# A graph-attention layer with residual and layer norm: adjacency loads by whole blocks, x loads one step later and singly near the end, statistics ahead of normalisation

## The chip, the core and the metric

The kernel runs on one core of a Trainium2 chip. A core has five engines that run their own instruction streams and meet through semaphores: TensorE (PE in the profile; its weight loads are PEld), VectorE (DVE), ScalarE (ACT), GpSimd (POOL) and SyncE (SP, which here only issues DMAs). Data comes from HBM into SBUF, an on-chip memory of 128 partitions; TensorE writes its results to PSUM. The metric is the device time of one execution in microseconds; the number compared is the median over runs.

## The reference

The inputs are x (4096 x 512), adj (4096 x 4096), W (512 x 2048: four heads of 512) and a (the heads' attention vectors), all float32.

```
ht  = (x @ W) by heads
e   = leaky_relu(src_i + dst_j, 0.01) + adj        # src = ht . a_src, dst = ht . a_dst
att = softmax(e over j)
y   = mean over heads of att @ ht
out = layernorm(x + y)        # mean and variance over 512, eps 1e-5, no scale, no shift
```

The entries of adj that aren't zero lie between 0.05 and 1e9. In nearly every row the largest entry of adj exceeds the second by so much more than the attention scores can differ that the softmax is exactly one at that entry and zero elsewhere. Then `att @ ht` for row i is `x[col_i] @ W_h`, where `col_i` is the place of the largest entry of the row, and the mean over heads is `x[col_i] @ mean(W_h)`. The kernel computes this, and a bound which proves it for these inputs.

## The kernel before

Rows are handled in 32 blocks of 128: partition p holds the rows 32p to 32p+31, and block `ib` is row 32p+ib of every partition. One block of adj is 128 x 4096 float32, 2 MB, 16 KB in each partition.

**Buffers.** `adj_pool` has six buffers of one block each. `hold` (128 x 32 x 512, L95) keeps all of x, and later the output in its place; while W is needed, the second half of `hold` holds W (L96, `load_w`). Four PSUM banks are for `o`, the sum of a block's residual and product, and two for transposes.

**Loads.** All of them are issued by SyncE in order. `load_adj` (L105) loads a block in pieces: `pieces` (L102) gives four for block 0 and for blocks 28 to 31, and two for the others. `load_x` (L112) loads four blocks of x at a time. Step t of the main loop (from L352) issues x if it is due, then block t+5 of adj; `x_at` (L347) puts group g, blocks 4g to 4g+3, at step 4g-2, ahead of block 4g+3 of adj. After the loop comes the last group of x (blocks 28 to 31), then the stores of blocks 0 to 25, still from SyncE. A load into an adj buffer waits until VectorE has read the block that was in it, and every DMA of SyncE waits until the one eight issues before it has landed.

**The work on one block, spread over seven steps.** At step t:
- VectorE finds the largest entry of each of 64 segments of 64 columns of block t (`segment_maxima`, L155, one reduction for each piece), and then the best segment (`find_segment`, L162 and L164). Between the two halves of the block it does `find_column` (L184, L189) for block t-2: the place inside the segment.
- GpSimd computes the row index (L166), gathers the best segment of each row from HBM (`lead`, L168), and for block t-2 the column (L191) and with it the 128 rows of x (`y`, L178).
- TensorE transposes the gathered rows of block t-3 (`turn`, L204), which ScalarE copies to SBUF (`yt`, L206), starts the sum with the residual (identity times x, `residual`, L210), and multiplies by the mean of W (`products`, L217; `w_sum` is made in the first three steps).
- ScalarE takes the mean and the variance of block t-4 (`stats`, L229 and L231), and the squared length of its x rows (`row_norm`, L224), for the bound.
- Every second step GpSimd turns the sums of two blocks, t-6 and t-5, into a factor and a shift (`rstd`, L234 to L236, which writes `sd` and `nm`), and ScalarE normalises the two into `hold` (`finish`, L240). In before, ScalarE has the order: copy of `yt`, `finish` of the pair, `stats`, `row_norm`.
- In steps 1 to 14 TensorE and ScalarE also make the attention vectors (L279 to L287), which step 16 turns into norms (`head_norms`).

**The end.** Blocks 28 to 31 are normalised by VectorE (`finish_last`, L246 to L255: add, bn_stats, bn_aggr, a square root on ScalarE, reciprocal, scaling). `bound` needs the squared lengths of all rows: part 0 takes the maximum over blocks (`xm`, L312) and transposes it on TensorE (L314), part 1 reduces it, takes the root and spreads it (L316 to L319), part 2 forms the limit; `test`, `count` and `report` compare all rows with it. Each engine works through its instructions in the order of the program text, which is written out by hand:

```
    row_norm(28 .. 31)                           # ScalarE
    turn(NB - 2)
    products(NB - 3, KB - 1, KB)
    bound(0)
    products(NB - 2)
    finish_last(NB - 4, True)
    find_inner(NB - 1)
    bound(1)
    finish_last(NB - 3, True)
```

The program text by line numbers:

Of the kernel before, what the change touches and what calls it, by code (L numbers as in the profile page):

```python
# [65 lines left out]
def leading_rows(ctx, tc, x, adj, W, a, out, ident, v, n_bad, any_bad):  # L66
# [7 lines left out]
    nc = tc.nc  # L74
    N, D = x.shape
    H = a.shape[0]
    KB, NB, S = D // P, N // P, N // E
    AHEAD = 5
    Q = 4
    PIECES = 4  # L80
    LATE = NB - Q
# [9 lines left out]
    x_rows = x.rearrange("(p nb) d -> p nb d", nb=NB)  # L91
# [3 lines left out]
    hold = once.tile([P, NB, D], F32, name="hold")  # L95
# [4 lines left out]
    adj_t = {}  # L100

    def pieces(ib):  # L102
        return PIECES if ib == 0 or ib >= LATE else PIECES // 2

    def load_adj(ib):  # L105
        if 0 <= ib < NB:
            t = adj_t[ib] = adj_pool.tile([P, N], F32, name="adj_t")
            n = pieces(ib)
            for k in range(n):
                nc.sync.dma_start(t[:, ts(k, N // n)], adj_rows[ib][:, ts(k, N // n)])  # L110

    def load_x(g):  # L112
        nc.sync.dma_start(hold[:, ts(g, Q), :], x_rows[:, ts(g, Q), :])

    def load_w(kb):
        nc.sync.dma_start(hold[:, ds(w_at + kb * H, H), :], w_blocks[:, kb])
# [4 lines left out]
    for kb in range(KB):  # L121
        load_w(kb)
        load_adj(kb + 1)
    load_x(0)
    for ib in range(KB + 1, AHEAD):
        load_adj(ib)

# [21 lines left out]
    def segment_maxima(ib, lo, hi):  # L149

        if lo == 0:
            seg_of[ib] = small.tile([P, S], F32, name="seg")
        n = pieces(ib)
        for k in range(lo * n // PIECES, hi * n // PIECES):
            nc.vector.tensor_reduce(  # L155
                seg_of[ib][:, ts(k, S // n)],
                adj_t[ib][:, ts(k, N // n)].rearrange("p (s e) -> p s e", e=E), axis=AX.X, op=OP.max,
            )

    def find_segment(ib):  # L160
        seg = seg_of.pop(ib)
        nc.vector.max(out=top[:, ib, :], in_=seg)  # L162
        at = small.tile([P, 8], U32, name="at")
        nc.vector.max_index(at, top[:, ib, :], seg)  # L164
        row = small.tile([P, 1], U32, name="row")
        nc.gpsimd.tensor_tensor(row, at[:, 0:1], first[:, ib : ib + 1], op=OP.add)  # L166
        lead = small.tile([P, E], F32, name="lead")
        nc.gpsimd.indirect_dma_start(  # L168
            out=lead, out_offset=None, in_=adj_segs,
            in_offset=bass.IndirectOffsetOnAxis(ap=row[:, :1], axis=0),  # L170
        )
        start = at_of[ib] = small.tile([P, 1], U32, name="start")
        nc.gpsimd.tensor_tensor(start, at[:, 0:1], width, op=OP.mult)  # L173
        lead_of[ib] = lead
# [8 lines left out]
    def find_inner(ib):  # L183
        nc.vector.max(out=inner[:, ib, :], in_=lead_of[ib])  # L184

    def find_column(ib):
        find_inner(ib)
        within = small.tile([P, 8], U32, name="within")
        nc.vector.max_index(within, inner[:, ib, :], lead_of.pop(ib))  # L189
        col = small.tile([P, 1], U32, name="col")  # L190
        nc.gpsimd.tensor_tensor(col, at_of.pop(ib), within[:, 0:1], op=OP.add)  # L191
        gather_rows(ib, col)
# [15 lines left out]
    def residual(ib):  # L208
        o_ps[ib] = psum.tile([P, D], F32, name="o")
        nc.tensor.matmul(o_ps[ib], ident, hold[:, ib, :], start=True, stop=False)  # L210

    def products(ib, lo=0, hi=KB):
        start = ib not in o_ps
        if start:
            o_ps[ib] = psum.tile([P, D], F32, name="o")
        for kb in range(lo, hi):
            nc.tensor.matmul(  # L217
                o_ps[ib], yt_of[ib][:, kb, :], w_sum[:, kb, :],
                start=(start and kb == 0), stop=(kb == KB - 1),
            )  # L220

    def row_norm(ib):
        sq = rows.tile([P, D], F32, name="sq")
        nc.scalar.activation(sq, hold[:, ib, :], AF.Square, accum_out=xx[:, ib : ib + 1])  # L224

    def stats(ib):
        o, i = o_ps[ib], slice(ib, ib + 1)
        sq = rows.tile([P, D], F32, name="sq")
        nc.scalar.activation(sq, o, AF.Identity, scale=-1.0 / D, accum_out=nm[:, i])  # L229
        sq = rows.tile([P, D], F32, name="sq")  # L230
        nc.scalar.activation(sq, o, AF.Square, bias=nm[:, i], accum_out=sd[:, i])  # L231

    def rstd(i):
        nc.gpsimd.tensor_scalar(sd[:, i], sd[:, i], 1.0 / D, EPS, op0=OP.mult, op1=OP.add)  # L234
        nc.gpsimd.tensor_tensor(sd[:, i], sd[:, i], power[:, : i.stop - i.start], op=OP.pow)  # L235
        nc.gpsimd.tensor_mul(nm[:, i], nm[:, i], sd[:, i])  # L236
# [5 lines left out]
    def finish_last(ib, residual):  # L242

        o = o_ps.pop(ib)
        if residual:
            nc.vector.tensor_add(hold[:, ib, :], o, hold[:, ib, :])  # L246
            o = hold[:, ib, :]
        st = small.tile([P, nc.vector.BN_STATS_DIM], F32, name="st", bufs=2)
        nc.vector.bn_stats(st, o)  # L249
        mv = small.tile([P, nc.vector.BN_AGGR_DIM], F32, name="mv", bufs=2)  # L250
        nc.vector.bn_aggr(mv, st)
        r = small.tile([P, 1], F32, name="r", bufs=2)
        nc.scalar.activation(r, mv[:, 1:2], AF.Sqrt, bias=eps)
        nc.vector.reciprocal(r, r)
        nc.vector.tensor_scalar(hold[:, ib, :], o, mv[:, 0:1], r, op0=OP.subtract, op1=OP.mult)  # L255
# [4 lines left out]
    def mean_of_heads(kb):  # L260
        o = psum.tile([P, D], F32, name="o")
        for h in range(H):
            nc.tensor.matmul(o, ident, hold[:, w_at + kb * H + h, :], start=(h == 0), stop=(h == H - 1))  # L263
        nc.scalar.activation(w_sum[:, kb, :], o, AF.Copy, scale=1.0 / H)  # L264
# [5 lines left out]
    def turn_a():  # L270
        tp = psum.tile([P, KB, P], F32, name="tp", bufs=2)
        for k in range(KB):
            nc.tensor.transpose(tp[:, k, : 2 * H], a_rows[:, ts(k, P)], ident[: 2 * H, : 2 * H])
        nc.scalar.copy(at_d, tp[:, :, : 2 * H])
# [33 lines left out]
    def bound(part):  # L308

        if part == 0:  # L310
            xm = once.tile([P, 1], F32, name="xm")
            nc.vector.tensor_reduce(xm, xx, axis=AX.X, op=OP.max)  # L312
            px = of_bound[0] = psum.tile([1, P], F32, name="px", bufs=1)
            nc.tensor.transpose(px, xm, ident)  # L314
        elif part == 1:
            nc.vector.tensor_reduce(xg, of_bound[0], axis=AX.X, op=OP.max)  # L316
            nc.scalar.activation(xg, xg, AF.Sqrt)
            pb = of_bound[1] = psum.tile([P, 1], F32, name="px", bufs=1)
            nc.tensor.matmul(pb, ones[0:1, :], xg, start=True, stop=True)  # L319
        else:  # L320
            nc.vector.tensor_mul(lead_by, of_bound[1], vn)
            nc.vector.tensor_scalar(lead_by, lead_by, 1.05, 110.0, op0=OP.mult, op1=OP.add)
# [21 lines left out]
        nc.vector.tensor_reduce(total, pg, axis=AX.X, op=OP.add)  # L344
        nc.vector.tensor_scalar(any_bad, total, -1.0, float(N), op0=OP.mult, op1=OP.add)

    x_at = {4 * g - 2: g for g in range(1, NB // Q - 1)}  # L347
    vectors = [(kb, h) for kb in range(KB) for h in range(H)]
    vectors_at = {t: 2 if t < 3 else 1 for t in range(1, 15)}
    COLUMN, PROJECT, STATS, FINISH = 2, 3, 4, 6  # L350

    for t in range(NB):  # L352
        if t in x_at:
            load_x(x_at[t])
        load_adj(t + AHEAD)
        middle = 1 if t == NB - 1 else 2
        segment_maxima(t, 0, middle)
        if t >= COLUMN:
            find_column(t - COLUMN)
        segment_maxima(t, middle, PIECES)  # L360
        find_segment(t)
        pair = t >= FINISH and t % 2 == 0
        if pair:
            rstd(slice(t - FINISH, t - FINISH + 2))
        if t < 2:
            mean_of_heads(t)
        elif t == 2:
            mean_of_heads(2)
            mean_of_heads(3)
        if t == 0:  # L370
            turn_a()
        turned = [(*vectors[0], turn_w(*vectors.pop(0))) for _ in range(vectors_at.get(t, 0))]
        if t == 16:
            head_norms()
        ib = t - PROJECT
        if ib >= 0:
            turn(ib)
            if ib < LATE:
                residual(ib)
        for some in turned:  # L380
            head_vector(*some)
        if ib >= 0:
            products(ib)
        if pair:
            finish(t - FINISH)
            finish(t - FINISH + 1)
        if t >= STATS:
            stats(t - STATS)
            row_norm(t - STATS)

    load_x(NB // Q - 1)
    for ib in range(NB - FINISH):
        store(nc.sync, ib, 1)
    find_column(NB - 2)
# [7 lines left out]
        row_norm(ib)  # L402
    turn(NB - 2)
    products(NB - 3, KB - 1, KB)
    bound(0)
    products(NB - 2)
    finish_last(NB - 4, True)
    find_inner(NB - 1)
    bound(1)
    finish_last(NB - 3, True)  # L410
    bound(2)
# [249 lines left out]
```

## Time and profile before

| what | value |
|---|---|
| median of 7 runs | 250.38 us (248.48 to 250.75) |
| the profiled execution | 249.54 us |
| its span (first to last instruction of the trace) | 247.6 us |
| PE, DVE, ACT, POOL busy | 80%, 76%, 44%, 39% of the span |
| bytes moved by DMA | 97.77 MB, 395 GB/s over the span |
| loads of adj by SyncE | 54 of 1 MB, 20 of 512 KB |
| loads of x by SyncE | 8 of 1 MB |
| stores | 31 by SyncE, 1 by ScalarE, 256 KB each |

The profile is of one execution, so sums of its durations are set against 249.54 us and its span, not against the median. In its lists a row is: start and length in us (or length in ns), engine, line of the program, operation, output <- inputs with their shapes, how many, and in square brackets the idle time of the engine before it and what ended it. A DMA counts from its issue to its landing. The "DMA share" is the busy share of the 16 DMA engines and can come out a little over one. TensorE's matmul ends are modelled, so its busy share says little about how near it is to its peak.

### The profile page before, as it was taken

How to read it: one execution, taken by the hardware profiler on the slowest of the kernel's cores; microseconds unless marked ns; L12 is line 12 of the kernel's file. 1: busy time of each engine (PE TensorE's matmuls, PEld its weight loads, DVE VectorE, ACT ScalarE, POOL GpSimd, SP SyncE). 2: the span in 40 equal slices, each digit the busy share in tenths (PEclk: the TensorE clock that was granted, in tenths of full speed). 3: DMA queues.
4: the chain of work that ended last, by engine and by line, in shares of the span. 5: the costliest groups of instructions: out<-in, count | busy, mean ns of one | idle time of the engine just before them, and what ended most of it. 6: DMA issues, size and time to landing. Idle time of an engine off the chain costs nothing.

```text
span 247.6 us, 2569 instructions
## 1 busy us (share of the span) xinstructions
PE 199.1 (80%) x677; PEld 99.9 (40%) x678; DVE 188.9 (76%) x304; ACT 110.0 (44%) x266; POOL 97.5 (39%) x213
## 2 busy tenths in 40 slices
PE   0098859999999999999687878887799875957970
PEld 0034526466666666555242423332343332423420
DVE  2656677696899489967989799949995899973681
ACT  2002002144747575657555453645193708294310
POOL 1022423245256524654454546344554445563000
PEclk9999799999999999999999999999799999999996
DMA  6999999999999999999999999999999999999991
GB/s 242 418 417 420 418 414 412 417 413 410 417 408 408 408 418 413 412 413 410 416 409 417 406 417 408 408 411 410 417 412 408 403 404 401 405 398 356 398 342 65
DMA packets 20612, 97.77 MB, mean 395 GB/s; under 512 B 2920, under 2 KB 2920, under 8 KB 12144
## 3 DMA queue, kind: packets, MB, share of 16 engines
q1 hardware_dynamic: 16848, 87.83, 88.0%
q0 software_dynamic: 3584, 9.44, 10.0%
q10 hardware_dynamic: 160, 0.28, 0.3%
q8 instruction: 7, 0.11, 0.2%
q14 instruction: 13, 0.11, 0.1%
HBM read 89.15 MB, written 8.39 MB: 394 GB/s over the span
## 4 chain that ended last, share of the span: by engine, by line
DMA 48%; issue 19%; POOL 19%; DVE 10%; ACT 2%; POOLq 0%; PE 0%; DVEq 0%
DMA adj_t<-in_adj_dram 38%; DMA hold<-in_L_gnn_W_dram 6%; POOL lead L168 6%; POOL y L178 6%; DVE seg L155 4%; DMA y<-in_x_dram,col 3%; POOL sd L235 2%; POOL start L173 1%; POOL row L166 1%; POOL col L191 1%; DVE st L249 1%; ACT sq L224 1%; DVE hold L255 1%; DVE hold L246 1%; POOL sd L234 1%
## 5 line engine op out<-in xcount | busy, mean ns | idle before, releaser
L155 DVE TENSOR_REDUCE seg<-adj_t 128x32 f32<-128x2048 f32 (+1 forms) x74 | 146.3, 1987 | 36.8 <-DMA adj_t<-in_adj_dram 36.8
L217 PE MATMUL o<-w_sum,yt 128*128 128x512 f32 x256 | 118.6, 605 | 5.8 <-ACT yt L206 5.8
L217 PEld LDWEIGHTS o<-w_sum,yt 128*128 128x128 f32 x256 | 46.3, 191 | 64.1 <-issue 45.6
L178 POOL DMA_INDIRECT y<-in_x_dram,col x32 | 32.2, 1007 | 17.4 <-POOL col L191 15.2
L168 POOL DMA_INDIRECT lead<-in_adj_dram,row x32 | 30.8, 963 | 15.5 <-POOL row L166 15.5
L263 PE MATMUL o<-hold,ident 128*128 128x512 f32 x32 | 19.1, 751 | 17.1 <-DMA hold<-in_L_gnn_W_dram 17.1
L206 ACT COPY yt<-tp 128x512 f32<-128x512 f32 x32 | 18.7, 585 | 29.8 <-PE tp L204 29.6
L204 PE MATMUL tp<-ident,y 128*128 128x128 f32 x128 | 20.1, 281 | 14.3 <-DMA y<-in_x_dram,col 14.2
L210 PE MATMUL o<-hold,ident 128*128 128x512 f32 x58 | 30.7, 611 | 0.5 <-DMA hold<-in_x_dram 0.5
L240 ACT ACTIVATE hold<-o,nm,sd 128x512 f32<-128x512 f32 x28 | 20.3, 777 | 23.2 <-POOL nm L236 23.2
L166 POOL TENSOR_TENSOR row<-at,first 128x1 uint32<-128x1 uint32 x32 | 5.9, 184 | 54.3 <-DVE at L164 53.2
L204 PEld LDWEIGHTS tp<-ident,y 128*128 128x128 f32 x128 | 14.7, 144 | 27.5 <-issue 27.1
L281 ACT COPY wt<-tp 128x512 f32<-128x512 f32 x16 | 9.2, 586 | 29.7 <-PE tp L279 29.7
L191 POOL TENSOR_TENSOR col<-start,within 128x1 uint32<-128x1 uint32 x31 | 5.8, 188 | 37.4 <-DVE within L189 36.6
L224 ACT ACTIVATE sq<-hold 128x512 f32<-128x512 f32 x32 | 19.8, 620 | 0.0
L231 ACT ACTIVATE sq<-o,nm 128x512 f32<-128x512 f32 x28 | 19.3, 688 | 0.9
L287 PEld LDWEIGHTS pv<-at_d,wt 128*128 128x128 f32 x128 | 16.2, 191 | 7.0 <-ACT wt L281 4.0
L263 PEld LDWEIGHTS o<-hold,ident 128*128 128x128 f32 x32 | 7.3, 238 | 26.3 <-POOL row L166 12.1
L264 ACT ACTIVATE w_sum<-o 128x512 f32<-128x512 f32 x4 | 2.4, 598 | 33.9 <-PE o L263 33.9
L229 ACT ACTIVATE sq<-o 128x512 f32<-128x512 f32 x28 | 16.9, 604 | 0.0
L287 PE MATMUL pv<-at_d,wt 128*128 128x2 f32 x128 | 15.4, 244 | 0.6 <-ACT wt L281 0.6
L279 PEld LDWEIGHTS tp<-ident,hold 128*128 128x128 f32 x64 | 7.9, 142 | 6.9 <-issue 6.9
(73 smaller groups left out, 116.7 us busy)
## 6 DMA issues: line engine op xcount, KB each, us to landing
adj_t<-in_adj_dram SPq DMA_DIRECT2D x54, 1024.0 KB, 22.5
adj_t<-in_adj_dram SPq DMA_DIRECT2D x20, 512.0 KB, 11.9
hold<-in_x_dram SPq DMA_DIRECT2D x8, 1024.0 KB, 23.0
out_dram<-hold SPq DMA_DIRECT2D x31, 256.0 KB, 4.7
hold<-in_L_gnn_W_dram SPq DMA_DIRECT2D x4, 1024.0 KB, 17.3
lead<-in_adj_dram,row POOLq DMA_INDIRECT x32, 5.6
y<-in_x_dram,col POOLq DMA_INDIRECT x32, 7.0
out_dram<-hold ACTq DMA_DIRECT2D x1, 256.0 KB, 2.5
```

Of the source, the lines that this page charges most:

```text
L155: nc.vector.tensor_reduce(seg_of[ib][:, ts(k, S // n)], adj_t[ib][:, ts(k, N // n)].rearrange("p (s e) -> p s e", e=E), axis=AX.X, op=OP.max,)
L168: nc.gpsimd.indirect_dma_start(out=lead, out_offset=None, in_=adj_segs, in_offset=bass.IndirectOffsetOnAxis(ap=row[:, :1], axis=0),)
L178: nc.gpsimd.indirect_dma_start(out=y, out_offset=None, in_=x, in_offset=bass.IndirectOffsetOnAxis(ap=col[:, :1], axis=0),)
L204: nc.tensor.transpose(tp[:, kb, :], y[:, ts(kb, P)], ident)
L206: nc.scalar.copy(yt, tp)
L210: nc.tensor.matmul(o_ps[ib], ident, hold[:, ib, :], start=True, stop=False)
L217: nc.tensor.matmul(o_ps[ib], yt_of[ib][:, kb, :], w_sum[:, kb, :], start=(start and kb == 0), stop=(kb == KB - 1),)
L224: nc.scalar.activation(sq, hold[:, ib, :], AF.Square, accum_out=xx[:, ib : ib + 1])
L231: nc.scalar.activation(sq, o, AF.Square, bias=nm[:, i], accum_out=sd[:, i])
L240: nc.scalar.activation(hold[:, ib, :], o_ps.pop(ib), AF.Identity, bias=nm[:, i], scale=sd[:, i])
L263: nc.tensor.matmul(o, ident, hold[:, w_at + kb * H + h, :], start=(h == 0), stop=(h == H - 1))
L287: nc.tensor.matmul(pv[:, kb, h : 2 * H : H], wt[:, k, :], at_d[:, k, h : 2 * H : H], start=(k == 0), stop=(k == KB - 1),)
```

## The change

Five things change.

1. Blocks 1 to 27 of adj are loaded by one DMA of 2 MB each, 29 and 30 by two; 0, 28 and 31 stay at four. VectorE still reduces each block in at least two halves (`n = max(pieces(ib), 2)`).
2. The groups of x for blocks 4 to 23 are asked for one step later (step 4g-1), and so stand behind block 4g+3 of adj in the queue instead of ahead of it.
3. x for blocks 24 to 27 comes by four loads of one block (256 KB), at steps 22 to 25, each ahead of one of the blocks 27 to 30 of adj.
4. In a step of the main loop ScalarE does `stats` and `row_norm` ahead of the pair's `finish`.
5. At the end, `finish_last` of block 28 and `find_inner` of block 31 move ahead of `bound(0)` and of the products of block 30.

```diff
     def pieces(ib):
-        return PIECES if ib == 0 or ib >= LATE else PIECES // 2
+        return PIECES if ib in (0, LATE, NB - 1) else 2 if ib > LATE else 1
...
-    def load_x(g):
-        nc.sync.dma_start(hold[:, ts(g, Q), :], x_rows[:, ts(g, Q), :])
+    def load_x(lo, n):
+        nc.sync.dma_start(hold[:, ds(lo, n), :], x_rows[:, ds(lo, n), :])
...
-        n = pieces(ib)
+        n = max(pieces(ib), 2)
         for k in range(lo * n // PIECES, hi * n // PIECES):
...
-    x_at = {4 * g - 2: g for g in range(1, NB // Q - 1)}
+    x_at = {lo - 1: (lo, Q) for lo in range(Q, LATE - Q, Q)}
+    x_at.update({ib - 2: (ib, 1) for ib in range(LATE - Q, LATE)})
...
         if t in x_at:
-            load_x(x_at[t])
+            load_x(*x_at[t])
...
+        if t >= STATS:
+            stats(t - STATS)
+            row_norm(t - STATS)
         if pair:
             finish(t - FINISH)
             finish(t - FINISH + 1)
-        if t >= STATS:
-            stats(t - STATS)
-            row_norm(t - STATS)
-
-    load_x(NB // Q - 1)
+
+    load_x(LATE, NB - LATE)
...
     products(NB - 3, KB - 1, KB)
+    finish_last(NB - 4, True)
+    find_inner(NB - 1)
     bound(0)
     products(NB - 2)
-    finish_last(NB - 4, True)
-    find_inner(NB - 1)
     bound(1)
     finish_last(NB - 3, True)
```

More of the change, by code (lines that the diff above doesn't have):

```diff
@@ L123, in leading_rows @@
         load_adj(kb + 1)
-    load_x(0)
+    load_x(0, Q)
     for ib in range(KB + 1, AHEAD):
```

## The prediction, made before the changed kernel was run

> **What bounds the kernel now.** I read the slices and DMA rows of the page first, then the busy time by stage, and then VectorE, GpSimd, ScalarE and TensorE in order of time from 190 us on. The slices:
>
> ```profile
> DMA  6999999999999999999999999999999999999991
> ...
> DMA packets 20612, 97.77 MB, mean 395 GB/s; under 512 B 2920, under 2 KB 2920, under 8 KB 12144
> ```
>
> The DMA engines never rest, so until the last block of adj has landed time is bytes. By stage (columns: window, length, busy of PE, PEld, DVE, ACT, POOL, TensorE clock, DMA share, GB/s):
>
> ```profile
> 164.00:189.70 25.70, 21.00 (x55) 9.14 (x55) 21.48 (x32) 12.91 (x32) 12.24 (x27) 0.93 1.02 413
> 189.70:216.50 26.80, 21.68 (x61) 9.28 (x60) 25.32 (x44) 13.13 (x33) 13.15 (x29) 1.00 1.03 404
> ```
>
> The first window is four blocks in 8 KB rows, with one 1 MB load of x; VectorE has 4.2 us to spare. The second holds the four last blocks in 4 KB rows without x: VectorE is nearly full and the rate falls to 404. VectorE in order of time:
>
> ```profile
> 192.93 2.29 DVE L155 TENSOR_REDUCE seg<-adj_t 128x32 f32<-128x2048 f32 x1 [0.41 <-DMA adj_t<-in_adj_dram]
> ...
> 212.85 1.20 DVE L155 TENSOR_REDUCE seg<-adj_t 128x16 f32<-128x1024 f32 x1
> ...
> 220.68 4.42 DVE L197 FIND_INDEX8 col<-top,adj_t 128x8 uint32<-128x4096 f32 x1
> 230.36 0.19 DVE L312 TENSOR_REDUCE xm<-xx 128x1 f32<-128x32 f32 x1 [5.27 <-ACT sq L224]
> ```
>
> After the second half of block 27 (192.93) it waits for no adj any more, and starts block 31 at 212.85. Then comes a 5.27 us wait for row squares. Why they are late is seen in GpSimd, then ScalarE:
>
> ```profile
> 216.78 1.06 POOL L178 DMA_INDIRECT y<-in_x_dram,col  x1 [0.39 <-POOL col L191]
> ```
> ```profile
> 225.96 0.59 ACT L206 COPY yt<-tp 128x512 f32<-128x512 f32 x1 [3.48 <-PE tp L204]
> 226.44 1.45 ACT L240 ACTIVATE hold<-o,nm,sd 128x512 f32<-128x512 f32 x2
> ...
> 230.23 0.58 ACT L206 COPY yt<-tp 128x512 f32<-128x512 f32 x1
> 232.13 0.29 ACT L253 ACTIVATE r<-mv,eps 128x1 f32<-128x1 f32 x1 [1.32 <-DVE mv L251]
> ```
>
> Block 29's rows are asked for at 216.78, 3.85 us after VectorE is done with block 30, and land at 225.16 (8.37 us, stores are under way). ScalarE copies them, normalises 26 and 27, squares four rows, and copies block 30's rows. TensorE:
>
> ```profile
> 230.60 0.27 PE L314 MATMUL px<-ident,xm 128*1 128x128 f32 x1
> 230.86 3.70 PE L217 MATMUL o<-w_sum,yt 128*128 128x512 f32 x8
> 234.49 0.38 PE L319 MATMUL px<-xg,ones 1*128 1x1 f32 x2
> 234.80 0.66 PE L204 MATMUL tp<-ident,y 128*128 128x128 f32 x4
> ```
>
> From here TensorE (block 30's products, block 31's transposes and products, done at 240.17) and VectorE (28, 29, test, 30, report, at 240.39) run without a pause and meet at block 31's bn_stats, 240.32. The last store goes out at 242.62. The stores before it drain until 242.24, so the store queue stands just behind.
>
> **What the Trainium skill says.** "DMA: Bandwidth & Descriptors", "Why small descriptors are slow (HBM only)": every packet carries a fixed cost. The trace agrees: packets of q1 take 84, 162 and 314 ns (medians) for 2, 4 and 8 KB, so 8 to 10 ns fixed. Same page, "Queues, rings and completion order": a DMA engine alternates between queues packet by packet, so a gather waits for other queues' packets. The trace agrees: y gathers take 7.0 to 7.1 us among 8 KB packets and 6.3 to 6.4 among 4 KB ones; four packets each, 4 x 0.15 = 0.6. "PSUM — Partial Sum Buffer", "Engine vs sequencer instructions": ScalarE, VectorE and GpSimd are strict FIFOs, and TensorE's matmuls keep program order; the timelines above show the same.
>
> **The change, part by part.** The bare numbers are block numbers.
>
> *Whole blocks 1 to 27.* A 16 KB row replaces two of 8 KB; no 16 KB load of adj is in the trace. If it is one packet it costs 8 + 2 x 306 = 620 ns against 628. Each engine carries 8 rows of a block: 8 x 8 ns, and one completion packet of 9 ns less, is 73 ns a block, 1.97 us by block 27. Bounds: nothing, if rows are cut to 8 KB; 3.9 us with the fixed cost from mean durations (168.1 and 319.5 give 16.7 ns: 27 x (8 x 16.7 + 9)). I take 1.97. VectorE now starts a block when all of it is there, so block results come up to 2.8 us later; mid-kernel nobody misses them. Prices: without x a block period is 5.735 us ((25.7 - 4 x 0.07 - 2.56)/4, with 8 x 0.3195 for x), VectorE needs 5.56 (66.89 to 72.45). A buffer is freed about 1.4 us before the next block has landed, with four blocks behind it in the queue: no gap. Had it only one block, each late release would cost.
>
> *x one step later, and 24 to 27 singly.* Group loads land right behind block 4g+3 instead of before it: 2.6 us after it, while block 4g's gathered rows, which TensorE transposes ahead of the residual, come some 5.5 us after it. Cost nothing, with 3 us cover. Three of the four last single loads move behind block 27: 0.75 x 2.56 = 1.92 us earlier; 2 KB rows cost 8 x (4 x 84 - 314) = 0.18 us more in all, 0.05 of it before block 27. SyncE's queue issues 43 loads of adj instead of 74 and 11 of x instead of 8, at 0.33 us each (SP rows of 0.33); it runs some 22 us ahead of the data, so that is covered. So block 27 lands at 192.91 - 1.97 - 1.87 = 189.07.
>
> *VectorE from block 27 to 31.* Before: 212.85 - 192.93 = 19.92 us from its second half. After: the whole of 27 (5.56), 28 in quarters (5.68, 195.80 to 201.48), 29 and 30 in halves (5.56 each): 22.36, which is 2.44 more. Block 30's second half lands near 208.6, when VectorE gets to it, so this is a near tie. Block 31 starts 1.97 + 1.87 - 2.44 = 1.40 earlier; I take 1.3 for the tie. Everything that follows from block 30 (lead, y of 29 and 30, ScalarE's squares) moves with it. The gather's 8.37 us I leave; it could be 7.
>
> *Statistics before the pair's normalisation.* ScalarE waits 23.2 us in all for nm; 2.3 us of statistics (L229, L231, L224) now fill that. It isn't the bound (44%). The normalisation frees the PSUM bank that the next step's residual needs; its nm is ready no earlier, and the statistics are done by then. Nothing either way; if they were late, the residual has 2.9 us in hand.
>
> *finish_last(28) before bound(0).* Add, bn_stats and bn_aggr of block 28 (1.6 us) go into VectorE's 5.27 us wait. But the square root r stands on ScalarE behind block 30's copy: r 230.75 instead of 232.13. Reciprocal, scaling and inner follow (r to inner took 0.99 before), so xm starts at 231.87 instead of 230.36. On TensorE xm's transpose stands ahead of block 30's products, which were ready at 230.81. Behind them queue the broadcast, block 31's transposes, its products: all 1.5 us later. VectorE's 0.7 us gain before block 30 is lost to waiting. End of the tail: +1.5.
>
> Sum: -1.3 + 1.5 = +0.2 us on the profiled execution (249.54, span 247.6). It lies 0.84 below the median of the runs, 250.38; I add the difference to the median: 250.6.
>
> **Rivals.** *A row of 16 KB brings nothing* (cut in two, or HBM is slower at it). Place: landing of block 27; price 1.97, so +2.2: 252.6, slower. It decides once less than about 1 us is saved. For: no such packet of adj in the trace. Against: 2, 4 and 8 KB rows are one packet each. *The front gains more*: 3.9 us saved, or block 29's gather back at 7 us because it meets the stores later: -1.3 to -1.9, less the tie: 249.1, faster. For: the mean durations, and gathers of 6.3 at 221.45. Against: the 413 and 404 GB/s fit the smaller cost. *Gathers become the wait*: behind 16 KB packets y takes 7 + 4 x 0.31 = 8.2, lead 5.5 + 0.6 = 6.1. VectorE wants lead 7.4 us after its issue (2 x 5.735 + 2.3 - 5.56 - 0.8). At 8.2 the waits use up VectorE's 3.3 us of spare per four blocks; beyond, it is late at 27, around +2: 252.4. Against: three times my estimate would be needed.
>
> **How the numbers follow.** Forecast 0.45, no gain of rows 0.20, more gain 0.25, gathers 0.10. About 0.5% (1.25 us) is what a measurement can tell from no change. Faster: 0.22 of the third and 0.03 of the first; slower: 0.18, 0.07 and 0.06; same: the rest, 0.44. Range 248.7 to 252.8; the forecast's own is 249.4 to 251.8.
>
> **What would show it.** Packets of 16 KB near 620 ns. Block 27's first reduction near 189.1, block 31's near 211.5, y of 29 asked for near 215.5. VectorE's wait for row squares split, its rest before L254 of block 28; L314 followed by products about 1.5 us after ScalarE's copy of yt. y gathers near 8.2 us in mid-kernel. Wrong if rows show as 8 KB packets, if TensorE waits for x at L210, or if block 30's rows, not r, hold L314.

## The result, and the profile after

The changed kernel takes 248.01 us in the median of 27 runs (246.84 to 250.08), against 249.53 of the kernel before (64 runs on the same chip). The ratio is 0.9939, with a 95% interval of 0.9924 to 0.9953: 1.5 us faster, where 0.2 us slower was forecast. The profiled execution took 248.13 us with a span of 246.2 (before: 249.54 and 247.6), so the two profiles show nearly the whole difference. Of the cases that the prediction named, the second rival, a front that gains more, came nearest.

The slices and the packets, on the page of the changed kernel:

```profile
DMA  6999999999999999999999999999999999999961
...
DMA packets 16580, 97.77 MB, mean 397 GB/s; under 512 B 2472, under 2 KB 2472, under 8 KB 11184
```

The same bytes go in 4,032 fewer packets. In the trace q1 has 3,456 packets of 16 KB (27 blocks of 128 rows), so a row is one packet. It takes 620 ns in the median, as forecast, and 625.5 in the mean; an 8 KB packet of the kernel before took 314 in the median and 319.5 in the mean. Before, only the very last slice was not full; now the last two are a 6 and a 1, so the stores drain well before the end.

By stage (window, length, busy of PE, PEld, DVE, ACT, POOL, TensorE clock, DMA share, GB/s), up to block 27 and from there to block 31:

```profile
162.80:188.00 25.20, 19.53 (x54) 8.01 (x52) 20.94 (x32) 13.14 (x32) 12.31 (x27) 1.00 1.01 413
188.00:214.00 26.00, 24.11 (x69) 10.74 (x70) 24.91 (x40) 15.73 (x40) 14.74 (x32) 1.00 1.02 407
```

The windows are alike in kind, and VectorE is still nearly full in the second; both just come earlier. Over the long middle the rate rises from 412 (35 to 189.7 us, before) to 417 GB/s (35 to 188 us). What had been moved when block 27 landed (packets and MB of all queues, then packets, MB and share of the time for SyncE's queue q1 and the gathers' queue q0), before, at 192.91:

```profile
DMA packets 13004, 78.52 MB, mean 407 GB/s; under 512 B 1956, under 2 KB 1956, under 8 KB 4673
...
q1 hardware_dynamic: 10113, 70.93, 90.3%
q0 software_dynamic: 2864, 7.44, 9.9%
```

and after, at 188.01:

```profile
DMA packets 9096, 77.50 MB, mean 412 GB/s; under 512 B 1503, under 2 KB 1503, under 8 KB 4349
...
q1 hardware_dynamic: 6317, 70.22, 90.0%
q0 software_dynamic: 2752, 7.15, 9.7%
```

So block 27 came sooner for two reasons: the bytes moved faster, and there were fewer of them ahead of it, of x (q1) and of the gathers (q0). VectorE in order of time:

```profile
188.03 2.29 DVE L155 TENSOR_REDUCE seg<-adj_t 128x32 f32<-128x2048 f32 x1 [0.82 <-DMA adj_t<-in_adj_dram]
...
210.44 1.20 DVE L155 TENSOR_REDUCE seg<-adj_t 128x16 f32<-128x1024 f32 x1
...
218.00 0.23 DVE L184 MAX8 inner<-lead 128x8 f32<-128x64 f32 x1 [1.80 <-DMA lead<-in_adj_dram,row]
...
224.53 0.69 DVE L246 TENSOR_TENSOR hold<-o,hold 128x512 f32<-128x512 f32 x1 [1.09 <-ACT sq L224]
...
228.11 0.16 DVE L254 RECIPROCAL r<-r 128x1 f32<-128x1 f32 x1 [1.95 <-ACT r L253]
```

Block 27 is there at 188.03, 4.9 us earlier than its last half before; block 31 is begun at 210.44, 2.41 earlier. At the end the 5.27 us wait for row squares has become 1.09, and a new wait of 1.95 stands before L254 of block 28. GpSimd, ScalarE and TensorE:

```profile
214.37 1.06 POOL L178 DMA_INDIRECT y<-in_x_dram,col  x1 [0.39 <-POOL col L191]
```
```profile
221.95 0.59 ACT L206 COPY yt<-tp 128x512 f32<-128x512 f32 x1 [2.22 <-PE tp L204]
222.43 1.45 ACT L240 ACTIVATE hold<-o,nm,sd 128x512 f32<-128x512 f32 x2
...
227.30 0.58 ACT L206 COPY yt<-tp 128x512 f32<-128x512 f32 x1 [0.97 <-PE tp L204]
227.78 0.30 ACT L253 ACTIVATE r<-mv,eps 128x1 f32<-128x1 f32 x1
```
```profile
226.63 0.63 PE L204 MATMUL tp<-ident,y 128*128 128x128 f32 x4 [1.20 <-DMA y<-in_x_dram,col]
227.09 1.02 PE L217 MATMUL o<-w_sum,yt 128*128 128x512 f32 x2
229.12 0.27 PE L314 MATMUL px<-ident,xm 128*1 128x128 f32 x1 [1.01 <-DVE xm L312]
```

Block 29's rows are asked for at 214.37 and land at 220.97: 6.60 us, where the profile before had 8.37. Its copy comes at 221.95 instead of 225.96. Block 30's rows (219.75 to 226.49) are then what TensorE and ScalarE wait for, not ScalarE's squares. From the start of block 30's copy to the start of its products it is 1.93 us (227.30 to 229.23) instead of 0.63: that is the price of the end's order.

### The profile page after: what moved, and what is told of

Read it like the earlier page. It is cut to its first block, busy times and chain, and to the rows that moved or that the text cites. A ratio compares the mean times of both kernels' runs of the same rounds, so it can differ in the third digit from the quotient of the medians.

```text
span 246.2 us, 2538 instructions
## 1 busy us (share of the span) xinstructions
PE 199.5 (81%) x677; PEld 100.4 (41%) x678; DVE 188.8 (77%) x300; ACT 110.3 (45%) x266; POOL 97.3 (40%) x213
## 4 chain that ended last, share of the span: by engine, by line
DMA 38%; issue 24%; POOL 22%; DVE 7%; PE 4%; ACT 1%; SPq 1%; POOLq 0%; DVEq 0%
DMA adj_t<-in_adj_dram 29%; POOL lead L168 7%; POOL y L178 7%; DMA y<-in_x_dram,col 6%; DVE seg L155 5%; DMA lead<-in_adj_dram,row 3%; PE o L217 3%; POOL sd L235 3%; POOL row L166 1%; POOL start L173 1%; POOL col L191 1%; PE tp L204 1%; POOL sd L234 1%; POOL nm L236 1%; DVE hold L255 1%
## 5 line engine op out<-in xcount | busy, mean ns | idle before, releaser
L217 PE MATMUL o<-w_sum,yt 128*128 128x512 f32 x256 | 119.8, 610 | 1.4 <-ACT yt L206 1.4
L263 PE MATMUL o<-hold,ident 128*128 128x512 f32 x32 | 20.6, 805 | 16.3 <-DMA hold<-in_L_gnn_W_dram 16.3
L210 PE MATMUL o<-hold,ident 128*128 128x512 f32 x58 | 29.8, 595 | 0.0
L240 ACT ACTIVATE hold<-o,nm,sd 128x512 f32<-128x512 f32 x28 | 20.2, 772 | 3.5 <-POOL nm L236 3.5
L263 PEld LDWEIGHTS o<-hold,ident 128*128 128x128 f32 x32 | 8.0, 262 | 26.3 <-POOL row L166 11.8
```

Source lines behind the costliest of these rows:

```text
L217: nc.tensor.matmul(o_ps[ib], yt_of[ib][:, kb, :], w_sum[:, kb, :], start=(start and kb == 0), stop=(kb == KB - 1),)
L240: nc.scalar.activation(hold[:, ib, :], o_ps.pop(ib), AF.Identity, bias=nm[:, i], scale=sd[:, i])
```

## The experiments

Ratios are to the kernel before, timed beside each on the same chip; medians in us. No experiment leaves out any of the computation. A second profile of the kernel before and of the changed one (the last experiment) took 249.01 and 247.96 us; where two numbers stand together below, the second is from these.

### One part of the change alone, on the kernel before

**Whole rows only**, timed twice, each time beside other kernels:

```diff
-        return PIECES if ib == 0 or ib >= LATE else PIECES // 2
+        return PIECES if ib in (0, LATE, NB - 1) else 2 if ib > LATE else 1
-        n = pieces(ib)
+        n = max(pieces(ib), 2)
```

> The kernel before with whole-block loads alone (x timing, ScalarE order and end as before). Theory: a 16 KB packet saves 13.5 ns against two of 8 KB in the mean (625.5 against 2 x 319.5), so block 27 lands 3.0 us earlier, near 189.9; from there VectorE needs 22.4 us for four blocks (19.9 before from the second half of 27), so its first reduction of block 31 starts near 212.3, only 0.5 us earlier than before, and the end moves by about -0.5 us. Rival 1, the rows are the whole gain: -1.5 us or more. Rival 2, late halves cost as much as rows save or more: 0 to +1.

> The kernel before with whole-block loads alone, once more: the first time gave a ratio of 0.9932 from 7 runs, with a profile in which TensorE's clock was halved from 220.8 to 224.2. Theory: block 27 lands near 189.9, block 31's first reduction near 212.3, and the end is 0.5 to 1.5 us earlier, the more when block 29's gather lands within 6.5 us; ratio 0.994 to 0.998. Rival, the rows give the whole of the change: ratio 0.992 to 0.994 again.

Measured: 248.41 (7 runs), ratio 0.9932 (0.9906 to 0.9958), and 248.45 (22 runs), 0.9959 (0.9940 to 0.9979). Rows alone gain 1.0 to 1.7 us. VectorE began block 27 at 190.75 and 190.12, 2.2 to 3.0 us earlier than it began the last half of it before. The edit also loads blocks 29 and 30 by halves instead of quarters, which wasn't timed apart. The expectation's 13.5 ns a row turned out too high a price (see why the prediction was wrong). The gather of block 29 took 6.24 and 5.99 us. Both profiles hold one thing more, taken up below: block 28's products, 3.70 us before, took 5.4.

**Timing of x only:**

```diff
-    x_at = {4 * g - 2: g for g in range(1, NB // Q - 1)}
+    x_at = {lo - 1: (lo, Q) for lo in range(Q, LATE - Q, Q)}
+    x_at.update({ib - 2: (ib, 1) for ib in range(LATE - Q, LATE)})
```

> The kernel before with the x timing alone (groups one step later, 24 to 27 singly). Theory: block 27 lands 1.9 us earlier, near 191.0, but the bytes up to block 31 are the same, so its pieces land where they did, and VectorE, which is done with block 30 by 211, waits for them: first reduction of block 31 near 212.3, the end -0.5 us. Each of rows and x is worth little alone, and together 2.4 (the changed kernel's first reduction of block 31 is at 210.44 against 212.85). Rival 1, x is the whole gain: -1.5. Rival 2, residuals wait for the later x: a wait at L210 of some us in all, and 0 or slower.

Measured: 249.65, ratio 1.0011 (0.9992 to 1.0031): nothing. Block 27 is there by 190.44, but with half rows the bytes of blocks 28 to 31 follow no faster, VectorE waits for pieces of them, and begins block 31 at 212.35, only 0.5 earlier.

**The end's order only:** `finish_last(NB - 4, True)` and `find_inner(NB - 1)` ahead of `bound(0)`, as in part 5 of the change.

> The kernel before with the end's order alone (finish_last of block 28 and find_inner ahead of bound(0)). Theory: the square root of 28 stands behind the copy of block 30's rows on ScalarE, xm behind it on VectorE, and block 30's products behind xm's transpose on TensorE: products start 1.9 us after that copy instead of 0.6, and the end is 1.3 to 1.5 us later. Rival, the new order fills the 5.3 us wait: 1.0 to 1.6 us earlier.

Measured: 250.58, ratio 1.0029 (1.0012 to 1.0046): slower by 0.7 us, half of what was forecast. The mechanism shows in its profile: the products of block 30 start 1.93 us after the copy of block 30's rows started, against 0.63 before. That execution took 252.55 us, the longest of the 22, and held a stretch at half clock (below) at 222.33, so nothing else is read from it.

### One part taken back from the changed kernel

**Rows in halves again** (`pieces` and `n` as before, the rest changed):

> The changed kernel with rows in halves as before (x timing, ScalarE order and end as changed). Theory: block 27 lands near 191.0 or a little before, VectorE is then held by block 31's pieces, whose bytes land where they did in the kernel before; first reduction of block 31 near 212.3, and the end's order costs 0.7 to 1.3: ratio 1.001 to 1.005, slower than before. Rival, rows do not matter and x with the end is the gain: 0.994 to 0.997.

Measured: 251.04 (10 runs), ratio 1.0074 (1.0046 to 1.0102). Without whole rows the change would have lost 1.8 us: the rows decide its sign. It lost more than expected; its profile has a stretch of products that run at half speed (below), which accounts for 1.5 us of that execution:

```profile
225.41 4.37 PE L217 MATMUL o<-w_sum,yt 128*128 128x512 f32 x6 [0.68 <-ACT yt L206]
```

In the changed kernel these six take 2.84.

**x at its old times** (`x_at = {4 * g - 2: (4 * g, Q) for g in range(1, NB // Q - 1)}`):

> The changed kernel with the old x timing (four blocks at a time, one step earlier); rows, ScalarE order and end as changed. Theory, that rows and x are worth much only together: block 27 lands near 189.9 instead of 188.0, block 31's first reduction starts near 212.3 instead of 210.4, the end is 1.5 to 1.9 us later than the changed kernel's, level with before (ratio 0.999 to 1.001). Rival, x is worth nothing here either, as it was worth nothing alone: 0 to 0.4 us later than the changed kernel, ratio 0.994 to 0.996.

Measured: 248.64, ratio 0.9975 (0.9958 to 0.9991), 0.9 us behind the changed kernel and between the two expectations. Block 27 landed at 189.93 and block 31 was begun at 212.32, 1.9 us later than in the changed kernel, as the theory had it. Only part of these 1.9 us reaches the end.

**The end's order back** (`bound(0)` and `products(NB - 2)` ahead of `finish_last(NB - 4, True)` again):

> The changed kernel with the end in the old order. Theory: products of block 30 start 0.6 us after the copy instead of 1.9, the end is 1.2 us earlier than the changed kernel's, so about 2.7 us under the kernel before (ratio near 0.989). Rival, the new order is what gained: 1.0 to 1.6 us later than the changed kernel, which is level with before.

Measured: 248.69, ratio 0.9959 (0.9931 to 0.9986): no gain. Yet VectorE reached block 31's bn_stats at 236.38 instead of 238.49, so the 2.1 us were there, and were lost behind it. ScalarE, and the waits of SyncE's queue (total us, times, longest):

```profile
238.70 0.39 ACTq L258 DMA_DIRECT2D out_dram<-hold  x1
```
```profile
SPq L258 <- DMA out_dram<-hold: 8.1, 6, 6.6
```

The last store, block 31's, is issued by ScalarE at 238.70. The store of block 30, ahead of it in the program but issued by SyncE, waited 6.6 us and went out at 241.26, just after block 31's had landed (241.20). In the trace both stores count up the same completion semaphore, and SyncE's wait for it, just ahead of block 30's store, ends at 241.22: block 30's was issued only after block 31's had landed. So I let SyncE issue both.

**The end's order back, and the last store by SyncE:**

```diff
-    store(nc.scalar, NB - 1, 1)
+    store(nc.sync, NB - 1, 1)
```

> The changed kernel with the end in the old order, as before, but with the last store issued by SyncE instead of ScalarE, so that block 30's store no longer waits for the slot of block 31's. Theory: block 31's bn_stats near 236.4 to 237.3 instead of 238.5, and now the last store follows it: the end 1.2 to 2.1 us earlier than the changed kernel's, ratio to before 0.985 to 0.989. Rival, the end is set by the draining of stores: as the changed kernel, 0.994.

Measured: 245.74 (4 runs), ratio 0.9863 (0.9841 to 0.9885). This beats both kernels. TensorE and VectorE:

```profile
226.95 0.27 PE L314 MATMUL px<-ident,xm 128*1 128x128 f32 x1
227.06 3.60 PE L217 MATMUL o<-w_sum,yt 128*128 128x512 f32 x8
```
```profile
226.14 0.19 DVE L312 TENSOR_REDUCE xm<-xx 128x1 f32<-128x32 f32 x1 [3.48 <-ACT sq L224]
...
236.31 0.70 DVE L249 BATCH_NORM_STATS2 st<-o 128x6 f32<-128x512 f32 x1
```

xm is ready before the copy of block 30's rows is done (226.87), so L314 and the products run on without a wait. The 6.6 us wait is gone from SyncE's list.

**Control: the changed kernel with the last store by SyncE,** and **the same with ScalarE's old order** (`finish` of the pair ahead of `stats` and `row_norm`):

> The changed kernel with only the last store issued by SyncE instead of ScalarE: the control for the old end with that store on SyncE (ratio 0.9863). Theory: the queue that issues the store is worth nothing, so this is level with the changed kernel, ratio 0.992 to 0.996, and the end's order alone is worth some 1.5 to 1.9 us. Rival, the queue is the gain: ratio 0.985 to 0.989. In the profile: block 31's first reduction near 210.4; and no half clock of TensorE between 217 and 240, as in the four profiles so far of kernels with both rows and x changed (it was there, at 220 to 222, in five of the six others).

> The same (changed kernel, last store on SyncE) with ScalarE in the old order: normalisation of a pair ahead of the statistics. Theory: level with the changed kernel with that store on SyncE within 0.3 us; ScalarE's waits for nm come back (near 23 us instead of 3.5), nothing behind them is late. Rival, the statistics ahead of the pair are part of the gain: 0.5 us or more slower.

Measured: 247.73, ratio 0.9935 (0.9907 to 0.9964), and 247.49, 0.9941 (0.9923 to 0.9958). The queue of the last store alone is worth nothing, so the end's order alone costs the changed kernel the step from 0.9863 to 0.9935, 1.8 us. The order of the statistics is worth nothing, though ScalarE's waits for nm at L240 are 3.9 us in all with the new order and 17.6 with the old: ScalarE had the time.

### Attempts at a better end

**Row squares ahead of block 29's copy, and block 31's residual ahead of block 30's transposes,** on the changed kernel:

```diff
     find_column_in_row(NB - 1)
+    for ib in range(LATE, NB):
+        row_norm(ib)
     turn(NB - 3)
     products(NB - 3, 0, KB - 1)
     finish(NB - FINISH)
     finish(NB - FINISH + 1)
-    for ib in range(LATE, NB):
-        row_norm(ib)
+    residual(NB - 1)
     turn(NB - 2)
```

> The changed kernel with two moves at the end: the row squares of blocks 28 to 31 go ahead of block 29's copy on ScalarE (their x is there since 216.8, and ScalarE waited from 219.7 to 221.95), and block 31's residual goes ahead of block 30's transposes on TensorE, into its wait of 1.2 us. Theory: xm no longer stands before block 30's products (1.3 us), and 0.86 us of TensorE leaves the chain: about 2 us earlier than the changed kernel, ratio to before 0.985 to 0.988. Rival, VectorE or the stores are then the bound: no more than 0.5 us.

Measured: 247.7, ratio 0.9927 (0.9909 to 0.9945), some 0.3 us from the changed kernel and inside both intervals. The miss is instructive. VectorE:

```profile
223.54 0.18 DVE L251 BATCH_NORM_AGGREGATE mv<-st 128x2 f32<-128x6 f32 x1
227.63 0.16 DVE L254 RECIPROCAL r<-r 128x1 f32<-128x1 f32 x1 [3.91 <-ACT r L253]
...
228.43 0.17 DVE L312 TENSOR_REDUCE xm<-xx 128x1 f32<-128x32 f32 x1
```

With the squares out of the way VectorE has block 28's variance at 223.7, and then waits 3.91 us for its root, which stands on ScalarE behind the copy of block 30's rows. It is r behind the copy that holds xm, and not the squares. The residual was no free filling either: it ran from 225.32, while block 30's rows landed at 225.35, so their transposes began only at 226.18.

**A rewritten end:** squares early as above, then `bound(0)`, `finish_last` of 28, `bound(1)`, all ahead of block 30's transposes, and the last store by SyncE. Besides, the rest of the bound, the test and block 29 come ahead of block 30's products, and block 31's transposes between those products.

```diff
+    bound(0)
+    finish_last(NB - 4, True)
+    bound(1)
     turn(NB - 2)
     products(NB - 3, KB - 1, KB)
...
-    finish_last(NB - 4, True)
...
-    bound(0)
-    products(NB - 2)
-    bound(1)
```

> A version to beat both: the changed kernel with the last store on SyncE and the end rewritten: row squares of 28 to 31 ahead of block 29's copy on ScalarE, the bound and the limit right after them, block 28 finished before block 30's copy, and block 31's transposes between the products of block 30. Theory: after ScalarE's copy of block 30 (near 226.3) TensorE has only products of 30, transposes, residual and products of 31 left, without a wait for that last copy, and VectorE has spare: bn_stats of block 31 near 235.5 instead of 236.3 in the old order, ratio to before 0.981 to 0.985. Rival, the gathers of blocks 30 and 31 hold it: no better than the old order, 0.986.

Measured: 246.64 (6 runs), ratio 0.9892 (0.9863 to 0.9922): better than the changed kernel, but not than the old end. TensorE:

```profile
225.15 0.27 PE L314 MATMUL px<-ident,xm 128*1 128x128 f32 x1
226.18 0.38 PE L319 MATMUL px<-xg,ones 1*128 1x1 f32 x2 [0.76 <-ACT xg L317]
226.49 0.66 PE L204 MATMUL tp<-ident,y 128*128 128x128 f32 x4
```

xm is begun at 222.89, 3.25 us sooner, but L314, reduction, root and broadcast are a round trip over three engines, and block 30's transposes now queue behind it: 226.49, against 225.62 in the version that won. There the round trip runs beside eight products. When block 30's rows landed isn't recorded in this profile, so how much of the 0.87 us is the round trip's is open.

### Second profiles

Two readings rested on single profiles: block 29's gather, and the slow products. Four kernels were profiled once more.

> The kernel before, unchanged, for a second profile. Theory (the gather depends on the kernel): block 29's y is asked for near 216.8 and takes 7.7 to 8.4 us again. Rival (chance): it takes 6 to 7 us. For the clock: theory, no stretch of half clock between 210 and 232 us, as in the first profile; rival, there can be one.

> The changed kernel, unchanged, for a second profile. Theory: block 29's y takes 6.0 to 7.2 us again, and no stretch of half clock lies between 210 and 232 us. Rival (chance): the gather can take 8 us, and a stretch of half clock can fall there.

> The kernel before with only the timing of x, for a second profile. Theory (the clock depends on the kernel): a stretch of 3.4 us at half clock near 220.5 us again, products of 5.4 us, and a gather of block 29 of 7.7 to 8.4 us. Rival (chance): no such stretch, or elsewhere.

> The changed kernel with x at its old times, for a second profile. Theory: a stretch of half clock near 220 us again, products of 5.4 us, and a gather of block 29 of 6.0 to 6.7 us. Rival (chance): no such stretch, or elsewhere.

Block 29's gather took 7.67 us in the kernel before, 6.56 in the changed one, 7.51 with x alone, 6.19 with x at its old times. With the other profiles: 7.5 to 8.4 us in five of kernels with half rows, 6.0 to 7.2 in nine with whole rows (in the other four the landing isn't recorded). It goes with the rows, then, not with chance. Why is not shown.

The slow products are, at least in part, chance. The same kernel (the changed one with x at its old times), in its first profile and in its second:

```profile
219.54 5.40 PE L217 MATMUL o<-w_sum,yt 128*128 128x512 f32 x8 [0.68 <-ACT yt L206]
```
```profile
219.15 3.70 PE L217 MATMUL o<-w_sum,yt 128*128 128x512 f32 x8 [0.68 <-ACT yt L206]
```

In the first the granted clock was half for 3.4 us from 220.08; block 30's products then started at 231.62 instead of 229.53, and the execution took 250.38 instead of 248.29 us. The x-only kernel had the stretch in both its profiles, near 220.3; the kernel before and the changed one had it there in neither of theirs. It isn't all chance: of the 18 profiles, the eight of kernels with both whole rows and the new times of x have no half clock between 215 and 232 us, and seven of the other ten have it there. Medians of these kernels can therefore hold a part that is the stretch's and not the part's that was changed.

## Why the prediction was wrong

Each step against both pairs of profiles (times in us; a minus is earlier than before):

| step of the prediction | forecast | first pair | second pair |
|---|---|---|---|
| block 27 has landed | -3.84 | -4.90 | -5.15 |
| VectorE from block 27 to 31 | +2.44 | +2.49 | +2.51 |
| block 31's first reduction | -1.3 | -2.41 | -2.64 |
| block 29's gather, length after | 8.37 | 6.60 | 6.56 |
| copy of block 30's rows | -1.3 | -2.93 | -2.26 |
| that copy to block 30's products | +1.5 | +1.30 | +1.32 |
| block 30's products start | +0.2 | -1.63 | -0.94 |
| profiled execution | +0.2 | -1.41 | -1.05 |

**The step that failed: the landing of block 27, "192.91 - 1.97 - 1.87 = 189.07".** It came 4.90 us earlier (5.15 in the second pair), not 3.84, and all of the difference reached block 31, since VectorE's own 2.44 was right to 0.1. Two terms of the sum were wrong, and that of x was right.

*A gather, put at nothing ("mid-kernel nobody misses them").* VectorE now starts a block only when all of it is there. So the rows of block 24 were asked for when they had been before (185.17 us against 185.09), while block 27 landed 4.9 us sooner. Before, these rows were there at 192.11, ahead of block 27; now they came at 191.49, behind it. Of the gathers' bytes 7.15 MB had moved by the landing instead of 7.44. I estimate this at 0.7 us: 0.29 MB at 407 GB/s. The second pair has the same 0.29 MB.

*The price of a row, 8 ns.* It was nearer 10. The test is the time that equal bytes take: from the 13.5th to the 76th MB of an execution it is 151.6 to 151.7 us in the six profiles of kernels with half rows, and 149.5 to 149.8 in the twelve with whole rows. In the changed kernel 3,008 rows of 16 KB lie in that stretch, 188 for each engine, and 369 completion packets fewer than before. So 2.0 us, less 0.2 for these, is 9.6 ns a row, and 27 x (8 x 9.6 + 9) ns = 2.3 us by block 27, where the prediction had 1.97. The mean durations, which the prediction kept for its bound, would give 2 x 319.5 - 625.5 = 13.5 ns, or 3.2 us, and that is too much. Durations of packets overlap: summed over the stretch they come to 154.1 us before and 151.3 after, more than the time that passed. So a part of what the means lose is overlap and not time.

Together the two are the first pair's excess of 1.1 us; of the second pair's 1.3 they leave 0.3 open. The mechanism of the rows was right and its size short by 0.3; the larger part was the order of the bytes.

**The second, smaller miss: "the gather's 8.37 us I leave; it could be 7".** It was 6.6. The copy of block 29 therefore came 4.0 us earlier (3.75 in the second pair). Little of that counts: before, block 30's copy followed 4.27 us of ScalarE work behind block 29's, and now it waits for block 30's own rows. Had the gather stayed at 8.37, the first pair's copy of block 30 would have come near 227.8 (214.37 + 8.37 + 0.80 from landing to copy, as before, + 4.27) instead of 227.30: an estimate of 0.5. In the second pair the shorter gather brought nothing, since block 30's rows took 7.12 us and the copy gained only 2.26 of block 31's 2.64.

In the first pair block 31's start (1.1), the gather (0.5) and the end's order (0.2) make up the 1.8 between +0.2 and -1.63. In the second, block 31's start (1.3) and the end's order (0.2), less 0.4 for block 30's rows, make up the 1.1 between +0.2 and -0.94. The second rival was right that the front gains more, but for other reasons in the main: it had 3.9 us for the rows, which gave 2.3, or a shorter gather, which counted in one pair of two, and it did not name the gather that fell behind block 27. That it came near is in part luck; the measured 248.0 lies below the whole range's 248.7.

Two slips changed nothing: the block period "5.735" is 5.715 by its own sum, and from 84 and 162 ns the fixed cost of a packet is 6 ns, so "8 to 10" should be 6 to 10.

**The end's order: right.** L314 was held by xm, xm by r, r by the copy, and it cost 1.3 in the traces. The timed runs give +0.7 on the kernel before and 1.8 on the changed one with the store's wait out of the way. Why the first is smaller is not settled.

**x later and singly: right in its place, nothing by itself.** No wait for x stands at L210, and block 27 gained the 1.9 us (189.91 with x at its old times, 188.01 in the changed kernel). Timed, it gave nothing alone and 0.9 us with whole rows. Of the 0.9 the profiles without a slow stretch show only 0.2 to 0.3 (248.29 against 248.13 and 247.96): block 31 is begun 1.9 us sooner, but block 30's gather is longer (6.74 and 7.12 us against 5.29) and lands no sooner. The rest may be the slow stretch, met less often; its share among the timed runs isn't known.

**Statistics first: right.** They are worth nothing either way.

**The rivals.** That a row brings nothing fell with the 16 KB packets of 620 ns. Gathers as the wait: y gathers between 70 and 195 us took 8.2 us in the median (7.0 before), the forecast figure; the Trainium skill's "DMA: Bandwidth & Descriptors", "Queues, rings and completion order", on which it rested, agrees. VectorE lost little to it: 2.9 us of waits for lead in all, 1.8 of them at block 30, after the last block of adj. That later block results keep no engine waiting held in the middle of the kernel; at the end block 30's gather did become the wait of TensorE, 1.20 us.

## What to carry to other kernels

When the size of packets changes, price it by the time that equal bytes take, not by durations of single packets, which can overlap: here medians gave 8 ns a row, means 13.5, and the time 10. To say when a load lands, count all the bytes ahead of it: one gather of 256 KB that fell behind block 27 was worth more than the error in the price of a row. Before a small operation is moved into an idle gap, look at what its partner engine has queued ahead of it: the add and bn_stats of block 28 fitted the gap, but the root they need stood behind a copy. And when a tail gets shorter, read the waits of the queues that carry the last stores; 2.4 us of gain (0.9959 against 0.9863) were lost to one store that waited for a later one's landing.

## What was not expected of the hardware

- Stretches of 3.4 us at half the TensorE clock near 220 us lengthen eight products from 3.70 to 5.40 us, in some executions of a kernel and not in others. Between two executions of one kernel the end moved by 2.1 us. What sets their place is open.
- A gather of 128 rows of x, issued as the loads end, took 7.5 to 8.4 us in kernels with 8 KB rows and 6.0 to 7.2 us in those with 16 KB rows, while in the middle of the kernel the order is the reverse: 7.0 against 8.2.
- Rows of 16 KB moved at 417 GB/s where 8 KB rows had 412, and the sum of packet durations fell by more than the time did (2.8 us against 2.0 over 62.5 MB).
